# Two chained cross attentions: a pair's first-batch image outputs as products and sums on GpSimd

## The chip, the core and the metric

The kernel runs on one core of a Trainium2 chip. The core has engines that work side by side, each with its own queue that it takes in order: TensorE (PE in the profile, its weight loads PEld), VectorE (DVE), ScalarE (ACT), GpSimd (POOL) and SyncE (SP), which here issues nearly all transfers (DMAs). They wait for one another by semaphores. TensorE writes into PSUM, a small memory that is handed out here in eight equal tiles of 2 KB per partition; the other operands lie in SBUF, which has 128 partitions. The metric is the device time of one execution in microseconds (us).

## The reference

There are 64 batches of 256 tokens with 320 channels (20 heads of 16 channels), and for each batch 77 context rows of 512, of which the last 4 are image tokens for the second layer.

```python
# layer 0: plain cross attention over the 77 rows (and an image part that has no rows here)
out_text = _merge_heads(_attend(q, k, v, sm_scale))
x = out @ Wo.T + bo + x
# layer 1: 73 text rows and 4 image rows
probs_t = softmax(q @ k_t * scale)
text_out = probs_t @ v_t
qsem = l2norm(probs_t @ text_ehs)
sem = qsem @ l2norm(ip_ehs).T
probs_ip = softmax(q @ k_ip * scale + 0.5 * sem) * spatial_mask
ip_out = probs_ip @ v_ip
out = (text_out + ip_out) @ W_out + b_out + x
```

The change concerns `ip_out = probs_ip @ v_ip` and its addition to `text_out`: for each token and head, four weights times four value rows of 16 channels.

## The kernel before

**Pairs and units.** Two batches make a pair; there are 32 pairs. The 20 heads are split into 16 main ones, which fill two times 128 channels, and 4 last ones (64 channels), which are kept apart. A batch is worked off in five units of 128 tokens by 8 heads, so a pair has ten units (`NU`). The main loop (L1098) runs over steps `g`; step `g` belongs to pair `p = g // 10`, and `k = g % 10` is the number of the step that this text uses (step 0 to step 9). In each step layer 0 works on unit `g` and layer 1 on unit `g - 13` (`LAG`). So while layer 0 works on pair `p`, layer 1 ends batch 0 of pair `p - 1` in step 9 of `p`, and its image part runs in the steps of `p + 1`. This is why calls in the list of work carry `p - 2`.

**The order in a step.** Work is emitted in this order: work held for this step (`early`, and the ends of projections); the matmuls of the scores into one PSUM tile of four banks, `sc` (pool `psc`, one buffer), for `semantics` (L760, L766), `scores` of both layers (L646); work called `begin`, with the image matmuls' copies in step 8; on DVE the maxima and subtractions of both layers (`shifted`, L664 and L666), then `middle`; the transposes of layer 1's weights (`transposed`); the exponential of layer 0; `weighted` on DVE (L777, L780), the last reader of `sc` but one; the list `first`; layer 0's transposes; `sums_out` on ACT (L1092), the last reader of `sc` (it stands ahead of layer 0's transposes in steps 1 and 8); the exponentials of layer 1 (L677, L678); `normalize` (DVE L692 and L693, then POOL L697, which makes `parts`, read by PE in the next step); `later`; at the end of a batch `text_output`; the lists `second`; `attend`; and `third`. `fillers(k, p)` puts the other work into these lists: `first`, `second`, `third` and `begin` are its lists 0, 1, 2 and 3.

`keep_order` makes PE, ACT, DVE and POOL take their instructions in the order in which they were written. SP is held to it only in the first 13 steps; after that the framework's scheduler orders SP's transfers by when it thinks that buffers come free, and may issue them early.

**PSUM.** Besides `sc` there are two pools of two tiles each: `ptr` (tag `tr`) for transposes and `pms` (tag `ms`) for matmuls. A third tile of a pool has to wait until a reader, mostly an ACT copy, is done with the first.

**The image part of layer 1.** When a batch ends, `text_output` scales the text outputs by head on POOL (L884) into `an` as [token, head, channel], the last four heads into `an_last`. In the steps after it come `image_scores`, `image_shifted`, `image_exponential` and `image_weights`, which give the weights `iw` as [token, half of the tokens, head, image token]. `text_transposed` turns `an` into channels by token on PE (L846) and copies it into `aT` (ACT, L848); this is in step 0 for batch 0 and in step 5 for batch 1. For the image outputs, `image_values` loads the four rows of `v_ip` sixteen times, once per head (`vip`, 16 transfers a batch, steps 7 and 8), `place_image_values` masks them by head on POOL (L483, step 9); `image_transposed` turns the weights of both batches into rows by token (PE, L948, four transposes into one `ptr` tile `itr`, and the ACT copy L950 into `iwT`, step 7); `image_attend` multiplies both (PE, L960, into two `pms` tiles `ipv`, step 8), copies them to SBUF (ACT, L970) and adds them to `aT` (POOL, L972). The last four heads are done otherwise: `last_image_values` loads the rows broadcast over all partitions (`vlast`), and `last_image_outputs` makes four products and four sums on POOL (L857, L860). `project(1, p - 2)` and `project_last(1, p - 3)` then read `aT`, in step 9 and in step 0.

Other work that the prediction names: `value_rows` (`v_ps`, PE L381, ACT copy `vs` L382) makes the value rows of a block of 128 context rows; `keys` and `last_keys` (`k_ps`, `kl_ps`, ACT copies L339 and L351); `gram` (its transfers `g_rest`, L515); `project_last(0, p - 1)` in step 2 ends with DVE's L625, for which PE's `last_queries` (L573, `q_ps`) waits; `image_least` (`least`, L897) squares the sums on POOL at the end of a batch. In the last steps, when there is no layer 0 any more, `keep_busy` has PE do transposes that nobody reads.

Of the kernel before, what the change touches and what calls it, by code (L numbers as in the profile page):

```python
# [15 lines left out]
D = 16  # L16
# [49 lines left out]
def tile_two_cross_attentions(ctx: ExitStack, tc: tile.TileContext, a: dict, out: bass.AP):  # L66
# [350 lines left out]
    def place_values(l, p, b):  # L417
# [51 lines left out]
            rest0[:n].rearrange("p (i g) -> p i g", g=4).unsqueeze(3).broadcast_to([n, 2, 4, D]), ALU.mult,  # L469
        )  # L470

    def image_values(p, b):


        n, r0 = HT * NIP, (2 * p + b) * NIP
        vip = vips[p, b] = big.tile([n, 2 * P], F32, tag="vip", name=f"vip{p}_{b}", bufs=3)
        for h in range(HT):
            nc.sync.dma_start(vip[h * NIP : (h + 1) * NIP, :], vip_rows[r0 : r0 + NIP, : 2 * P])

# [345 lines left out]
    def text_output(p, b):  # L825

        sums = stats[p, b][1]
        rec = small.tile([P, 2 * H], F32, tag="rec", name=f"rec{p}_{b}", bufs=2)
        nc.vector.reciprocal(rec, sums[:, :, NIP + D])
        an = big.tile([P, 2, HT, D], F32, tag="an", name=f"an{p}_{b}", bufs=1)  # L830
        if b == 0:
            lasts[p] = big.tile([P, 2, 2, H - HT, D], F32, tag="an_last", name=f"an_last{p}", bufs=1)
        by_head(an, lasts[p][:, :, b], sums[:, :, NIP : NIP + D], rec)
        return an

    def text_transposed(p, b):

        an = made["an"]
        if b == 0:
            aTs[1, p] = channels("aT1", f"aT1_{p}", 1)  # L840
        main = aTs[1, p][0]
        for s in range(2):
            ps = ptr.tile([P, 4, P], F32, tag="tr", name=f"atr{p}_{b}{s}")
            t = an[:, s].rearrange("p h d -> p (h d)")
            for i in range(2):
                nc.tensor.transpose(ps[:, i, :], t[:, i * P : (i + 1) * P], ident)  # L846
            t0 = b * S + s * P
            nc.scalar.copy(main[:, :, t0 : t0 + P], ps[:, :2])  # L848

    def last_image_outputs(p, b):  # L850

        v = vips[p, b, "last"].rearrange("p t (h d) -> p t h d", d=D)
        w, to = weights[p, b, "last"], lasts[p][:, :, b]
        part = [P, 2, H - HT, D]
        for t in range(NIP):
            prod = small.tile(part, F32, tag="ip_last", name=f"ip_last{p}_{b}{t}", bufs=1)
            nc.gpsimd.tensor_tensor(  # L857
                prod, v[:, t].unsqueeze(1).broadcast_to(part), w[:, :, :, t].unsqueeze(3).broadcast_to(part), ALU.mult
            )
            nc.gpsimd.tensor_add(to, to, prod)  # L860
# [81 lines left out]
    def image_transposed(p):  # L942
        n = HT * NIP
        ps = ptr.tile([P, 4, P], F32, tag="tr", name=f"itr{p}")
        for b in range(2):
            w = weights[p, b].rearrange("p s h t -> p s (h t)")
            for s in range(2):
                nc.tensor.transpose(ps[:n, 2 * b + s, :], w[:, s], ident)  # L948
        wT = big.tile([n, S2], F32, tag="iwT", name=f"iwT{p}", bufs=1)
        nc.scalar.copy(wT, ps[:n].rearrange("p j t -> p (j t)"))  # L950
        return wT

    def image_attend(p):

        wT = made["wT"]
        both = [pms.tile([P, 512], F32, tag="ms", name=f"ipv{p}_{i}") for i in range(2)]
        for b in range(2):
            for i in range(2):
                rows = slice(i * QR, (i + 1) * QR)
                nc.tensor.matmul(  # L960
                    both[i][:, b * S : (b + 1) * S], vips[p, b][rows, i * P : (i + 1) * P],
                    wT[rows, b * S : (b + 1) * S], start=True, stop=True,
                )

        def out_of(i):
            main = aTs[1, p][0]
            if p == NP - 1:
                nc.vector.tensor_add(main[:, i, :], both[i], main[:, i, :])
                return
            nc.scalar.copy(t[:, i, :], both[i])  # L970
            if i:
                nc.gpsimd.tensor_add(main, t, main)  # L972

        t = big.tile([P, 2, S2], F32, tag="ip_out", name=f"ip_out{p}", bufs=1)
        return [lambda i=i: out_of(i) for i in range(2)]


# [2 lines left out]
    def fillers(k, p):  # L980
# [4 lines left out]
        def add(half, q, fn, *args):  # L985
            if 0 <= q < NP:
                f[half].append((fn, args))

        if k == 0:
# [3 lines left out]
                add(1, p, values, 0, p, 0)  # L993
            add(0, p - 1, gram, p - 1, 0)
            add(0, p - 3, project_last, 1, p - 3)
            add(2, p - 2, text_transposed, p - 2, 0)
            if p:
                add(2, p, place_values, 0, p, 0)
            add(2, p - 1, values, 1, p - 1, 0)
        elif k == 1:  # L1000
# [3 lines left out]
                add(1, p, place_values, 0, p, 0)  # L1004
            add(0, p - 1, project, 0, p - 1)
            add(1, p - 2, last_image_values, p - 2, 0)
            add(1, p - 1, place_gram, 0)
            add(1, p, keys_by_head, 0, p, 1)
            add(1, p - 1, keys_by_head, 1, p - 1, 0)
        elif k == 2:  # L1010
# [6 lines left out]
            add(2, p - 1, lambda: made["q"]())  # L1017
            add(1, p - 1, place_values, 1, p - 1, 0)
            add(1, p, values, 0, p, 1)
        elif k == 3:  # L1020
            add(0, p + 1, load_context, p + 1)
            add(0, p, lambda: last_queries(0, p)())
            if p == 0:
                add(1, p, image_keys, 0)
            add(1, p - 1, queries, 1, p - 1)
            add(1, p, place_values, 0, p, 1)
            add(1, p - 1, keys_by_head, 1, p - 1, 1)
        elif k == 4:
            if p == 0:
                add(0, p, image_keys, 1)  # L1030
            else:
                add(0, p, keys, 1, p, 0)
            add(1, p - 1, values, 1, p - 1, 1)
            add(1, p - 2, last_image_outputs, p - 2, 0)
            add(1, p + 1, queries, 0, p + 1)
        elif k == 5:
            if p == 0:
                add(0, p, image_keys, 2)
            add(0, p + 1, keys, 0, p + 1, 0)
            add(1, p - 1, gram, p - 1, 1)  # L1040
            add(2, p - 2, text_transposed, p - 2, 1)
            add(1, p - 2, last_image_values, p - 2, 1)
        elif k == 6:
            while len(made_rows) * P < min(NB, 2 * (p + 2)) * T:
                rows_todo.extend((len(made_rows), l) for l in range(2))
                made_rows.append(rows_todo[-1])
            for n in range(len(rows_todo) // 2):
                add(0, p, value_rows, *rows_todo.pop(0))
            if p == 0:
                add(0, p, image_norms)  # L1050
            else:
                add(1, p, keys, 1, p, 1)
            add(1, p, place_image_keys, p)
        elif k == 7:
            add(0, p + 1, keys, 0, p + 1, 1)
            add(1, p + 1, last_keys, p + 1)
            add(1, p - 2, lambda: made.update(wT=image_transposed(p - 2)))
            add(1, p - 2, last_image_outputs, p - 2, 1)
            add(1, p - 1, image_values, p - 1, 0)
            if p == 0:  # L1060
                add(1, p, image_rows)
        elif k == 8:
            while rows_todo:
                add(0, p, value_rows, *rows_todo.pop(0))
            add(1, p - 1, place_gram, 1)
            add(1, p + 1, keys_by_head, 0, p + 1, 0)
            add(1, p - 1, image_values, p - 1, 1)
            add(1, p - 1, place_values, 1, p - 1, 1)
            add(1, p - 2, last_transposed, p - 2)
            add(3, p - 2, lambda: held.update(i=lambda: image_attend(p - 2)))  # L1070
        else:
            add(0, p - 2, project, 1, p - 2)
            add(1, p + 1, values, 0, p + 1, 0)
            for b in range(2):
                add(1, p - 1, place_image_values, p - 1, b)
        return f

    rows_todo, made_rows = [], [0, 1]
# [19 lines left out]
    for g in range(NP * NU + LAG + 12):  # L1098
# [39 lines left out]
            new1 = (*last1, pts[1])  # L1138
        if now[0] and k != 5:
            exponential(0, g, *now[0])  # L1140
        if before1:
            prod = weighted(ps, *before1[:4])
        if g - NP * NU in (18, 19):
            keep_busy(6)
        for fn, args in first:
            fn(*args)
        if before1 and k in (1, 8):
            sums_out(ps)
        if last0:
            transposed(0, *last0)  # L1150
# [6 lines left out]
            keep_busy(8)  # L1157
        if now[0] and k == 5:
            exponential(0, g, *now[0])
        if before1 and k not in (1, 8):  # L1160
            sums_out(ps)
        if now[1]:
            exponential(1, g, *now[1])
# [4 lines left out]
        if before1:  # L1168
            q, b, u = before1[:3]
            nc.vector.tensor_reduce(eight(stats[q, b][2], u), prod, AX.X, ALU.add)  # L1170
            if ends:
                image_squares(q, b)
                made["an"] = text_output(q, b)
                later[g + 1] = [(image_scores, (q, b))]
                middle[g + 2] = (image_shifted, (q, b))
                later[g + 2] = [(image_exponential, (q, b))]
                early[g + 3] = [(image_weights, (q, b))]
        for fn, args in second:
            fn(*args)
        if last0:  # L1180
# [63 lines left out]
```

## Time and profile before

| what | value |
|---|---|
| time, median of 3 runs | 2580.65 us (2578.83 to 2582.64) |
| the profiled execution, its own time | 2582.37 us |
| its span in the profile | 2580.6 us |
| granted TensorE clock, mean | 0.996 |
| one pair of batches in the middle (1193.8 to 1270.0 us) | 76.2 us |
| in it, busy: PE, DVE, ACT, POOL | 75.5, 60.7, 46.8, 51.7 us |

In the profile a line such as `L697 POOL ... parts<-w,sm` names the engine, the line of the kernel, what is written and what is read. Groups have their total busy time, the mean length of one in ns, and the idle time of the engine just ahead of them with what ended it. The chain of work is followed back from the last instruction, at each step to what released it. In the list of waits a line gives who waited for whom, the total in us, how often, and the longest. Ends of matmuls are modelled, so PE can look busy while it is held up.

### The profile page before, as it was taken

Reading aid. Unit: us, or ns where it says so; the run is one execution under the profiler, and the core shown is the slowest. Engines: PE = TensorE matmul, PEld = TensorE weight load, DVE = VectorE, ACT = ScalarE, POOL = GpSimd, SP = SyncE. Lnnn points to the kernel's source line nnn. Section 1 sums busy time; section 2 is a strip of 40 time slices with the busy share of each in tenths; the row PEclk is TensorE's granted clock in tenths of the full one; section 3 lists DMA queues with packets and bytes.
Section 4 is the critical chain, followed back from the end, with each engine's and each line's share of the span. In section 5 each row is a group of like instructions: output and inputs, shape, how many; then the busy total and the mean of one; then the engine's idle time right before and its main releaser. Section 6 shows DMA issues by size and latency. Waiting matters only on the chain.

```text
span 2580.6 us, 74528 instructions
## 1 busy us (share of the span) xinstructions
PE 2514.9 (97%) x27178; PEld 2010.2 (78%) x27178; DVE 1954.0 (76%) x3609; ACT 1510.1 (59%) x3893; POOL 1653.7 (64%) x4026
## 2 busy tenths in 40 slices
PE   7999999999999999999999999999999999999898
PEld 6677778777787777788777787777787777787676
DVE  4577777878777778777777777777777777777764
ACT  3465665665665665566665566656565665566543
POOL 3466666676666676666666666666666666666653
PEclk9999999999999999999999999999999999999999
DMA  5212211122211121212122212122211122211000
GB/s 166 58 45 61 62 46 47 49 59 55 63 45 49 48 59 54 64 44 52 45 59 54 64 45 52 45 58 54 67 44 48 45 60 54 62 41 41 26 25 27
DMA packets 186405, 138.33 MB, mean 54 GB/s; under 512 B 81016, under 2 KB 164728, under 8 KB 186040
## 3 DMA queue, kind: packets, MB, share of 16 engines
q1 hardware_dynamic: 185176, 132.41, 19.0%
q8 instruction: 217, 3.56, 0.6%
q14 instruction: 148, 1.21, 0.2%
q10 hardware_dynamic: 864, 1.15, 0.1%
HBM read 95.56 MB, written 33.91 MB: 50 GB/s over the span
## 4 chain that ended last, share of the span: by engine, by line
PE 68%; DVE 16%; ACT 4%; POOL 3%; DMA 3%; SPq 3%; issue 3%; DVEq 0%; POOLq 0%; ACTq 0%
PE sc L760 10%; PE q_ps L537 8%; PE tr L710 8%; PE sc L646 6%; DVE w L666 5%; PE v_ps L381 4%; DVE mx L664 4%; PE o_ps L537 4%; PE sc L766 4%; PE k_ps L336 4%; PE q_ps L546 3%; DVE prod L777 2%; PE pv L794 2%; DVE x L606 2%; PE pv L799 2%
## 5 line engine op out<-in xcount | busy, mean ns | idle before, releaser
L664 DVE TENSOR_REDUCE mx<-sc 128x8 f32<-128x584 f32 (+1 forms) x640 | 497.2, 777 | 439.3 <-PE sc L646 439.2
L697 POOL TENSOR_TENSOR parts<-w,sm 128x512 f32<-128x512 f32 (+1 forms) x640 | 440.5, 710 | 370.1 <-DVE sm L693 194.2
L666 DVE TENSOR_TENSOR w<-sc,mx 128x616 f32<-128x616 f32 x640 | 511.9, 800 | 66.6 <-ACT kT L339 0.5
L710 PE MATMUL tr<-ident,parts 128*128 128x128 f32 x2560 | 408.4, 282 | 8.1 <-POOL parts L697 3.8
L717 ACT COPY pt<-tr 128x512 f32<-128x512 f32 x320 | 187.5, 586 | 378.9 <-PE tr L710 376.2
L760 PEld LDWEIGHTS sc<-gv,pt 64*128 64x128 f32 x5120 | 319.5, 187 | 71.9 <-ACT sums L1092 44.1
L710 PEld LDWEIGHTS tr<-ident,parts 128*128 128x128 f32 x2560 | 284.9, 141 | 115.8 <-issue 71.4
L760 PE MATMUL sc<-gv,pt 64*128 64x94 f32 x5120 | 353.1, 277 | 12.8 <-ACT sums L1092 10.3
L674 ACT ACTIVATE w<-w 128x616 f32<-128x616 f32 x320 | 231.0, 722 | 151.9 <-DVE w L666 143.0
L692 DVE TENSOR_REDUCE sm<-w 128x8 f32<-128x616 f32 x320 | 250.9, 784 | 13.9 <-ACT w L674 13.9
L646 PE MATMUL sc<-kbd,q 32*128 32x154 f32 x5120 | 248.4, 306 | 1.0 <-ACT q L591 1.0
L537 PE MATMUL q_ps<-x,wq 128*128 128x256 f32 x1024 | 233.5, 381 | 3.3 <-ACT kT L339 3.3
L537 PE MATMUL o_ps<-aT,wo 128*128 128x256 f32 x1024 | 232.6, 380 | 0.0
L1170 DVE TENSOR_REDUCE nrm<-prod 128x8 f32<-128x584 f32 x320 | 227.1, 710 | 0.4
L777 DVE TENSOR_TENSOR prod<-sc,parts 128x512 f32<-128x512 f32 x320 | 217.9, 681 | 4.0 <-PE sc L766 4.0
L1092 ACT COPY sums<-sc 128x168 f32<-128x168 f32 x320 | 96.5, 302 | 199.8 <-DVE prod L780 198.9
L537 PEld LDWEIGHTS q_ps<-x,wq 128*128 128x128 f32 x1024 | 190.0, 191 | 27.6 <-ACT kT L339 4.3
L537 PEld LDWEIGHTS o_ps<-aT,wo 128*128 128x128 f32 x1024 | 190.3, 191 | 23.5 <-issue 0.2
L677 ACT ACTIVATE parts<-w 128x512 f32<-128x512 f32 x320 | 207.2, 647 | 0.0
L646 PEld LDWEIGHTS sc<-kbd,q 32*128 32x128 f32 x5120 | 187.0, 186 | 5.9 <-issue 4.8
L736 ACT COPY pt<-tr 128x512 f32<-128x512 f32 x256 | 150.1, 586 | 63.0 <-PE tr L710 62.7
L381 PE MATMUL v_ps<-wv,cf 128*128 128x320 f32 (+1 forms) x624 | 182.1, 438 | 0.0
(147 smaller groups left out, 4788.0 us busy)
## 6 DMA issues: line engine op xcount, KB each, us to landing
vip<-vip_rows SPq DMA_DIRECT2D x1024, 4.0 KB
out_dram<-x SPq DMA_DIRECT2D x64, 256.0 KB
x<-in_x_dram SPq DMA_DIRECT2D x31, 512.0 KB
v_rows<-vs SPq DMA_DIRECT2D x38, 320.0 KB
vm<-v_rows SPq DMA_DIRECT2D x152, 80.0 KB
ct<-in_ctx_dram SPq DMA_DIRECT2D x32, 308.0 KB
cf<-in_ctx_dram SPq DMA_DIRECT2D x38, 256.0 KB
g_rest<-gram_rest SPq DMA_DIRECT2D x512, 0.5 KB
```

The lines of the kernel that those rows point to most:

```text
L381: nc.tensor.matmul(ps[:n, :C], cfs[i][:, k, :n], wv[l][:, k, :], start=(k == 0), stop=(k == KE - 1))
L537: nc.tensor.matmul(ps[b][:, m, :], w[:, k, m * P : (m + 1) * P], main[:, k, b * S : (b + 1) * S], start=(k == 0 and m == 0), stop=False,)
L646: nc.tensor.matmul(ps[:, r, 2 * T * l : 2 * T * (l + 1)], q[rows, b, :] if part == 2 else q[rows, t0 : t0 + P], kbd[rows, part].rearrange( ...
L664: nc.vector.tensor_reduce(mx, sc[:, :, :, :nt], AX.X, ALU.max)
L666: nc.vector.tensor_tensor(w, sc, mx.unsqueeze(3).broadcast_to([P, 4, 2, T]), ALU.subtract)
L674: nc.scalar.activation(w, w, AF.Exp, scale=SCALE)
L692: nc.vector.tensor_reduce(sm, w, AX.X, ALU.add)
L697: nc.gpsimd.tensor_tensor(two[:, 8 * t0 : 8 * t1].rearrange("p (h t) -> p h t", h=8), w[:, :, t0:t1], sm.unsqueeze(2).broadcast_to([P, 8, ...
L710: nc.tensor.transpose(ps[:, i, :], flat[:, i * P : (i + 1) * P], ident)
L760: nc.tensor.matmul(ps[:, i % 2 * 2 + j, at : at + GV], pt[half_rows, i, :], gv[b][half_rows, part, i, :], start=start and i < 2, stop=False,)
L777: nc.vector.tensor_tensor(prod[:, :, :, :M], sm[:, :, :, :M], w[:, :4].rearrange("p (e a) j t -> p (a j) e t", e=2), ALU.mult)
L1170: nc.vector.tensor_reduce(eight(stats[q, b][2], u), prod, AX.X, ALU.add)
```

## The change

For batch 0 of each pair, the image outputs of the 16 main heads are no longer made by matmuls. `head_values` loads one row of `v_ip` broadcast over 128 partitions (`vt`, two buffers, 128 KB a load, four loads a pair). `head_products` multiplies it on POOL by the weights of that image token, over [token, half, head, channel] (128x512), and `head_sum` adds the product to `an`. This goes on in steps 2, 3 and 4: token 0 and its sum early in step 2, the product of token 1 at the end of step 2, sum 1, product 2, sum 2 and product 3 in step 3, sum 3 in step 4. `an` has two buffers, since batch 0's is now kept until step 7, where `text_transposed` of batch 0 comes (before, step 0); `aT` is now opened by batch 1 in step 5. `last_image_outputs` of batch 0 does two image tokens in step 4 and two in step 5, and `last_image_values` of batch 1 moves behind them. `image_values`, `place_image_values`, `image_transposed` and `image_attend` are left for batch 1 alone. Two orders change besides: in step 2 the list `first` runs ahead of `weighted`, and in step 6 `sums_out` runs ahead of layer 0's transposes.

```diff
+    def head_values(p, t):
+        r = 2 * p * NIP + t
+        v = vips[p, 0, t] = small.tile([P, 2 * P], F32, tag="vt", name=f"vt{p}_{t}", bufs=2)
+        nc.sync.dma_start(v, vip_rows[r : r + 1, : 2 * P].broadcast_to([P, 2 * P]))
...
-        vip = vips[p, b] = big.tile([n, 2 * P], F32, tag="vip", name=f"vip{p}_{b}", bufs=3)
+        vip = vips[p, b] = big.tile([n, 2 * P], F32, tag="vip", name=f"vip{p}_{b}", bufs=2)
...
-        an = big.tile([P, 2, HT, D], F32, tag="an", name=f"an{p}_{b}", bufs=1)
+        an = big.tile([P, 2, HT, D], F32, tag="an", name=f"an{p}_{b}", bufs=2)
...
-        return an
+        ans[b] = an
+
+    ans = {}
+
+    def head_products(p, t):
+        full = [P, 2, HT, D]
+        prod = made["ip"] = big.tile(full, F32, tag="ip_out", name=f"ip{p}_{t}", bufs=1)
+        nc.gpsimd.tensor_tensor(
+            prod, vips[p, 0, t].rearrange("p (h d) -> p h d", d=D).unsqueeze(1).broadcast_to(full),
+            weights[p, 0][:, :, :, t].unsqueeze(3).broadcast_to(full), ALU.mult,
+        )
+
+    def head_sum():
+        nc.gpsimd.tensor_add(ans[0], ans[0], made["ip"])
 
     def text_transposed(p, b):
-        an = made["an"]
-        if b == 0:
+        an = ans[b]
+        if b == 1:
             aTs[1, p] = channels("aT1", f"aT1_{p}", 1)
...
-    def last_image_outputs(p, b):
+    def last_image_outputs(p, b, tokens=range(NIP)):
...
-        for b in range(2):
-            w = weights[p, b].rearrange("p s h t -> p s (h t)")
-            for s in range(2):
-                nc.tensor.transpose(ps[:n, 2 * b + s, :], w[:, s], ident)
-        wT = big.tile([n, S2], F32, tag="iwT", name=f"iwT{p}", bufs=1)
-        nc.scalar.copy(wT, ps[:n].rearrange("p j t -> p (j t)"))
+        w = weights[p, 1].rearrange("p s h t -> p s (h t)")
+        for s in range(2):
+            nc.tensor.transpose(ps[:n, s, :], w[:, s], ident)
+        wT = big.tile([n, S], F32, tag="iwT", name=f"iwT{p}", bufs=1)
+        nc.scalar.copy(wT, ps[:n, :2].rearrange("p s t -> p (s t)"))
...
-        for b in range(2):
-            for i in range(2):
-                rows = slice(i * QR, (i + 1) * QR)
-                nc.tensor.matmul(
-                    both[i][:, b * S : (b + 1) * S], vips[p, b][rows, i * P : (i + 1) * P],
-                    wT[rows, b * S : (b + 1) * S], start=True, stop=True,
-                )
+        for i in range(2):
+            rows = slice(i * QR, (i + 1) * QR)
+            nc.tensor.matmul(both[i], vips[p, 1][rows, i * P : (i + 1) * P], wT[rows, :], start=True, stop=True)
...
         if k == 0:
-            add(2, p - 2, text_transposed, p - 2, 0)
...
         elif k == 1:
+            for t in range(2):
+                add(1, p - 2, head_values, p - 2, t)
...
         elif k == 2:
+            add(2, p - 2, head_products, p - 2, 1)
+            add(2, p - 2, head_values, p - 2, 3)
         elif k == 3:
...
+            add(1, p - 2, head_sum)
+            add(1, p - 2, head_products, p - 2, 2)
+            add(1, p - 2, head_sum)
+            add(1, p - 2, head_products, p - 2, 3)
         elif k == 4:
...
-            add(1, p - 2, last_image_outputs, p - 2, 0)
+            add(1, p - 2, head_sum)
+            add(1, p - 2, last_image_outputs, p - 2, 0, range(2))
...
         elif k == 5:
...
             add(2, p - 2, text_transposed, p - 2, 1)
-            add(1, p - 2, last_image_values, p - 2, 1)
+            add(2, p - 2, last_image_outputs, p - 2, 0, range(2, NIP))
+            add(2, p - 2, last_image_values, p - 2, 1)
...
         elif k == 7:
...
             add(1, p - 2, lambda: made.update(wT=image_transposed(p - 2)))
             add(1, p - 2, last_image_outputs, p - 2, 1)
-            add(1, p - 1, image_values, p - 1, 0)
+            add(2, p - 2, text_transposed, p - 2, 0)
...
-            for b in range(2):
-                add(1, p - 1, place_image_values, p - 1, b)
+            add(1, p - 1, place_image_values, p - 1, 1)
...
+        if k == 2:
+            for fn, args in first:
+                fn(*args)
         if before1:
             prod = weighted(ps, *before1[:4])
...
-        if before1 and k in (1, 8):
+        if before1 and k in (1, 6, 8):
             sums_out(ps)
...
+                if b == 0:
+                    early[g + 3] += [(head_products, (q, 0)), (head_sum, ()), (head_values, (q, 2))]
```

More of the change, by code (lines that the diff above doesn't have):

```diff
@@ L854, in last_image_outputs @@
         part = [P, 2, H - HT, D]
-        for t in range(NIP):
+        for t in tokens:
             prod = small.tile(part, F32, tag="ip_last", name=f"ip_last{p}_{b}{t}", bufs=1)
@@ L955, in image_attend @@
         wT = made["wT"]
-        both = [pms.tile([P, 512], F32, tag="ms", name=f"ipv{p}_{i}") for i in range(2)]
-        for b in range(2):
-            for i in range(2):
-                rows = slice(i * QR, (i + 1) * QR)
-                nc.tensor.matmul(
-                    both[i][:, b * S : (b + 1) * S], vips[p, b][rows, i * P : (i + 1) * P],
-                    wT[rows, b * S : (b + 1) * S], start=True, stop=True,
-                )
+        both = [pms.tile([P, 512], F32, tag="ms", name=f"ipv{p}_{i}")[:, :S] for i in range(2)]
+        for i in range(2):
+            rows = slice(i * QR, (i + 1) * QR)
+            nc.tensor.matmul(both[i], vips[p, 1][rows, i * P : (i + 1) * P], wT[rows, :], start=True, stop=True)
         def out_of(i):
-            main = aTs[1, p][0]
+            main = aTs[1, p][0][:, :, S:]
             if p == NP - 1:
-                nc.vector.tensor_add(main[:, i, :], both[i], main[:, i, :])
+                nc.vector.tensor_add(main[:, i], both[i], main[:, i])
                 return
@@ L972, in out_of @@
                 nc.gpsimd.tensor_add(main, t, main)
-        t = big.tile([P, 2, S2], F32, tag="ip_out", name=f"ip_out{p}", bufs=1)
+        t = big.tile([P, 2, S], F32, tag="ip_out", name=f"ip_out{p}", bufs=1)
         return [lambda i=i: out_of(i) for i in range(2)]
@@ L1144, in tile_two_cross_attentions @@
             keep_busy(6)
-        for fn, args in first:
-            fn(*args)
-        if before1 and k in (1, 8):
+        if k != 2:
+            for fn, args in first:
+                fn(*args)
+        if before1 and k in (1, 6, 8):
             sums_out(ps)
@@ L1159, in tile_two_cross_attentions @@
             exponential(0, g, *now[0])
-        if before1 and k not in (1, 8):
+        if before1 and k not in (1, 6, 8):
             sums_out(ps)
@@ L1172, in tile_two_cross_attentions @@
                 image_squares(q, b)
-                made["an"] = text_output(q, b)
+                text_output(q, b)
                 later[g + 1] = [(image_scores, (q, b))]
```

## The prediction

> **What bounds the kernel now.** I read the page's busy shares and its chain first, then the chain and each engine's timeline over one pair of batches in the middle (1194 to 1270 us), then the waits and the groups by shape.
>
> ```profile
> PE 2514.9 (97%) x27178; PEld 2010.2 (78%) x27178; DVE 1954.0 (76%) x3609; ACT 1510.1 (59%) x3893; POOL 1653.7 (64%) x4026
> PE 68%; DVE 16%; ACT 4%; POOL 3%; DMA 3%; SPq 3%; issue 3%; DVEq 0%; POOLq 0%; ACTq 0%
> ```
>
> TensorE (PE) is the bound on average, but the chain is only 68% PE, so steps differ. A step begins with its first `sc` matmul, and the starts of these groups give the steps' lengths, medians over pairs 4 to 30, steps 0 to 9: 8.02, 7.69, 7.91, 9.29, 8.58, 6.42, 6.82, 6.88, 6.75, 7.82 us. Every other pair repeats them within a few hundredths, except where a step carries a second block of value rows (steps 6 and 8, up to 8.58 and 8.90, in about one pair of five).
>
> There are two kinds of step. In the short ones (5, 6, 8) the only `sc` tile is held until VectorE (DVE) has read it for the fifth time and ScalarE (ACT) has copied the sums: 2.1 us of `sc` matmuls, 3.9 of DVE, 0.3 of ACT and gaps, about 6.5. In the others PE has more than that to do. Step 7 of the next pair, in the chain, is PE from end to end:
>
> ```profile
> 1277.40 1.13 PE sc L760 x16
> 1278.54 0.38 PE sc L766 x8
> ...
> 1281.79 1.05 PE kl_ps L346 x8
> 1282.85 0.51 PE itr L948 x4
> 1283.35 0.57 PE pv L794 x8
> 1283.92 0.43 PE pv L799 x8
> 1284.36 1.06 PE sc L760 x16
> ...
> 1286.38 0.85 PE ipv L960 x8
> ```
>
> The columns are start, length, what. `itr` is the image weights' transposes and `ipv` the image matmuls; the change halves both. ACT at the end of the same step 7, one pair earlier:
>
> ```profile
> 1207.41 0.30 ACT L1092 COPY sums<-sc 128x168 f32<-128x168 f32 x1 [0.71 <-DVE prod L780]
> 1207.61 0.64 ACT L677 ACTIVATE parts<-w 128x512 f32<-128x512 f32 x1
> 1208.15 0.25 ACT L678 ACTIVATE parts<-w 128x72 f32<-128x72 f32 x1
> 1208.31 0.57 ACT L351 COPY kl<-kl_ps 64x154 f32<-64x154 f32 x2
> 1208.90 0.58 ACT L950 COPY iwT<-itr 64x512 f32<-64x512 f32 x1
> ```
>
> ACT has no gap from 1207.41 on, and the copy that empties `itr` ends near 1209.48, while PE has gone into step 8 at 1208.15. Today nobody in step 7 minds that.
>
> **The change, part by part.** I count per pair, from 1201.27 (step 7's `sc`) on.
>
> *Step 7, PE.* Half of `itr` goes: 0.51 / 2 = 0.25 us. Four transposes of the first batch come at the end of the step (0.59 us, the `atr` row below). That alone makes +0.34. But the transposes need two PSUM tiles of the pool `ptr`, which has two slots: `transposed` of layer 0 takes both, `itr` the first that comes free, the first `atr` tile the other, and the second `atr` tile the slot of `itr`. So PE waits in its queue until ACT has done the `iwT` copy. That such a wait is real in this kernel is seen in the other two-slot pool:
>
> ```profile
> PEld v_ps L381 <- ACT ip_out L970: 6.1, 29, 0.2
> ```
>
> The `v_ps` matmuls have no data from `ip_out`; they wait 29 times for the slot. When does `iwT` end? What stands ahead of it on ACT is unchanged: sums (bound to DVE's `prod`, which ends 6.09 after `sc`), two exponentials, two `kl` copies; so it starts at 1208.90 again. Its length at 64x256 is not in the trace: between 0.29 (half of 579 ns) and 0.58 (as now); I take 0.37, since copies of 128x256 take 366 to 390 ns (L818, L869). So 1209.27; 0.05 for the semaphore; two transposes and the change of weights 0.45 (four take 0.59, of which 0.17 is the gap ahead of `sc`). Step 8 starts at 1209.77 instead of 1208.15: +1.62. PE would have arrived at this transpose near 1208.25, so about 1.05 of it is waiting. Queued behind it on PE is the next `sc`, and behind that all of DVE's chain.
>
> *Step 6's copies.* `sums_out` moves ahead of layer 0's transposes. In 6 the sums wait for DVE anyway (0.30 us idle), so nothing comes earlier; the two `pt`/`pr` copies and the exponentials come 0.7 us later. ACT idles 1.74 us before step 7's `pt` copy, which hides this; only the exponential of the image scores lies near a reader (`imx`, DVE) and may cost 0 to 0.08. I put 0.03. Step 7: +1.65, with bounds +0.34 and +1.95.
>
> *Step 8.* Half of `ipv` goes (0.43 PE), the ACT copies `ip_out` fall from 1.07 to some 0.6, and the GpSimd (POOL) addition L972 from 2.37 to 1.28. The step is bound by the `sc` chain: 6.75 now against 6.5 to 6.55, because the `vs` copy holds ACT 0.2 us past `prod`. So −0.20; in the fifth of pairs with two row blocks it is PE's, −0.43. Mean −0.25 (0 to −0.43).
>
> *Step 0.* Text transposes of the first batch leave it.
>
> ```profile
> 1230.16 0.66 PE L846 MATMUL atr<-ident,an 128*128 128x128 f32 x4
> 1230.75 1.13 PE L760 MATMUL sc<-gv,pt 64*128 64x94 f32 x16
> 1244.74 0.62 PE L799 MATMUL pv<-pr,vr 104*32 104x256 f32 x8
> 1245.71 0.66 PE L573 MATMUL q_ps<-x,wq 128*64 128x128 f32 x8 [0.35 <-DVE x L625]
> ```
>
> The sums of that step were out at 1229.94, so `sc` was ready 0.8 us before PE: the whole 0.59 is gained. Step 1 behind it has PE work without a gap, with 0.9 us between its sums and the next `sc`, so it passes the gain on.
>
> *Step 2.* `first` runs before `weighted`, so DVE does L625 before `prod`, and PE's 0.35 us before `q_ps` goes. `prod` and the sums come 0.40 later (1245.98 against PE's 1245.95): −0.30, between 0 and −0.35.
>
> *POOL.* Added: four products and four sums of 128x512.
>
> ```profile
> L697 POOL TENSOR_TENSOR parts<-w,sm 128x512 f32<-128x512 f32 x320 | 336.5, 1051 | 370.1 <-DVE sm L693 194.2 <-ACT parts L678 122.6 <-ACT gram L506 38.3
> L860 POOL TENSOR_TENSOR an_last<-an_last,ip_last 128x128 f32<-128x128 f32 x256 | 116.9, 457 | 20.1
> L972 POOL TENSOR_TENSOR aT<-ip_out,aT 128x1024 f32<-128x1024 f32 x31 | 73.4, 2369 | 1.4 <-ACT ip_out L970 1.4
> ```
>
> A product by L697 is 1.05. A sum lies on the line through L860 and L972: 457 + 384 × 2.13 = 1.28. Together 9.3; off come 1.1 of L972 and one L483 (0.6): +7.6, from 51.7 to 59.3 us of 76.2. Place by place: in step 2 POOL is done with the image weights at 1244.0 and `parts` starts at 1246.76, so 2.33 fit with 0.2 for `att`; the product behind the placed values ends near 1252.6, before `parts` at 1253.61; in step 3, POOL idles 4.43 us from 1257.7 to 1262.1, where two products and two sums take 4.7. There `least` and `parts` may come 0.3 late; PE needs these `parts` at 1267.7, so nothing. Step 4 swaps four small operations (1.9 us) for one sum (1.3); in step 5 they stand in the idle 2.15 before L921. Cover for all of it is PE's distance of a step to each `parts`; were it gone, each microsecond late is one.
>
> POOL work does not slow DVE: 347 of `w` (L666) ran beside a POOL instruction and 175 beside none, 800 ns both; `sm` (L692) took 784 both ways. L901, whose two tensors both lie in SBUF, takes 345 beside POOL and 200 without. The Trainium skill, "SBUF — State Buffer", section "Who interferes with whom", says a DVE instruction with two SBUF inputs contends with a GpSimd instruction that reads SBUF, one with at most one such input not; by it, too, only L901 would be touched. Against moving such work speaks "GPSIMD Engine Reference", section "Engine selection": two-input elementwise work is some 2 times slower there than on VectorE. By that, an estimate, the eight take 2 x 681 ns (`prod`, 128x512, on DVE), 10.9 us in place of 9.3; the rows (1051 to 681) say 1.5 times for the product, and the sum goes by the rows.
>
> *Queues.* SP loses 16 `vip` issues (8 take 3.13 us, so 6.3) and gains four (1.6). The first two loads have free buffers since step 3 of the pair before. Loads of tokens 2 and 3 wait for products at about 1245.1 and 1252.6, and are needed near 1259 and 1261. A load like it (`vlast`, issued at 1213.35) has its last packet at 1216.37, 3.0 us. `last_image_values` waits a step longer, to about 1199.7, behind eight `g_rest` issues (to 1204.5), lands by 1207.7 and is read at 1209.8. Cost 0, if SP's order is the program's. SP is not held to that order.
>
> *Tail.* POOL's small operations of step 5 now stand before L921 (+0.9), the transposes are on the path (+0.6), half of `ipv` goes (−1.1): +0.4 once.
>
> Sum: 1.65 − 0.25 − 0.59 − 0.30 = +0.51 per pair; 30 pairs run step 7 in full, +15.3, and the tail: +15.7. The profiled execution took 2582.37 (span 2580.6), so it would take 2598; it lies 1.7 above the median of the runs, which gives 2580.65 + 15.7 = 2596.
>
> **The rivals.**
> *No slot wait, faster.* If the `iwT` copy is no hindrance (ACT gets to it earlier, or the tile gets another slot), step 7 grows by 0.34 and the sum is −0.80 a pair, −24: 2557. It decides below a growth of 1.14 in step 7, that is where `iwT` is out 0.5 us earlier. For it: PE's gains are plain rows. Against: two slots, and ACT without a gap from the sums to `iwT`.
> *They cancel.* The wait is half of what I say, or DVE takes up more of it in step 8: −5 to +5.
> *A load comes late, slower still.* If SP issues `vlast` behind the `kl` transfers (1209.9), it lands at about 1213; POOL starts step 7's last outputs 3 us late, and PE's `ltr` in step 8, which by then has 2.1 us of margin, waits some 1 us: +30, 2627. For it: SP already waits 401 us at L489 for `ip_last`. Against: it has work before `kl`.
> *POOL becomes the bound.* At 59.3 of 76.7 us it isn't; only a place could be too tight, and the tightest (step 3) has 3.6 us to PE.
>
> **How the numbers follow.** My forecast has 0.60 and its own range is 2586 to 2608 (step 7 between +1.3 and +1.95). No slot wait 0.21, cancelling 0.08, late load 0.11. A measurement here tells about 0.2% (5 us) from none. Faster is the second case and a little of the third, 0.22; same 0.09; slower 0.69. A range that leaves out no more than 2 in 10 takes in half of the faster case and ends above the forecast's own: 2556 to 2612.
>
> **What would show it.** Right: step 7 near 8.5 us with a PE wait of about 1 us at `atr`, ended by `iwT`; step 8 near 6.5, step 0 near 7.4, step 2 near 7.6 with no wait for L625. Wrong: `atr` starting right behind `pv`; POOL's products waiting for a `vt` load; `sc` waiting for POOL's `least` chain.

## The result, and the profile after

The changed kernel takes 2600.5 us (median of 4 runs, 2597.46 to 2602.34) against 2581.64 us (4 runs, 2578.83 to 2583.97) of the kernel before: a ratio of 1.0078, with a 95% interval of 1.0063 to 1.0093. It is slower by 0.8%. The prediction was 2596 us, in a range of 2556 to 2612. The profiled execution took 2602.34 us with a span of 2600.6, that is 20.0 us more span than before.

The page of the changed kernel, busy shares and chain (lines of the code moved by 6 to 28: L760 is now L766, L897 is L918):

```profile
PE 2497.0 (96%) x26986; PEld 1993.9 (77%) x26986; DVE 1954.7 (75%) x3609; ACT 1496.2 (58%) x3893; POOL 1899.5 (73%) x4250
PE 56%; DVE 20%; ACT 10%; POOL 5%; DMA 4%; issue 3%; SPq 2%; DVEq 0%; POOLq 0%; ACTq 0%
```

TensorE (PE) has 18 us less to do and GpSimd (POOL) 246 us more, yet neither sum gives the time. The shift in the chain points to where it comes from: PE's share falls from 68% to 56%, and ScalarE's (ACT) rises from 4% to 10%. PE waits for ACT at places where it had work before.

The steps, measured from the first `sc` matmul of one to that of the next, show where. The medians are over pairs 4 to 30; the last column adds up the differences of the two profiled executions over steps `g` = 20 to 319.

| step | before, us | after, us | after less before, all pairs, us |
|---|---|---|---|
| 0 | 8.02 | 7.27 | −21.5 |
| 2 | 7.91 | 7.60 | −8.8 |
| 4 | 8.58 | 8.58 | −5.4 |
| 5 | 6.42 | 6.42 (six of 7.4 to 10.3) | +16.4 |
| 7 | 6.88 | 8.41 | +46.3 |
| 8 | 6.75 | 6.59 | −7.4 |
| 1, 3, 6, 9 | 7.69, 9.29, 6.82, 7.82 | the same | −0.1 |

The start adds 1.7 and the end takes 1.3: together 20 us. Step 7 alone costs more than the change gains elsewhere, and its PE timeline shows how (start, length, instruction; in brackets the idle time and who ended it):

```profile
750.90 0.38 PE L968 MATMUL itr<-ident,iw 128*64 128x128 f32 x2
751.21 0.64 PE L800 MATMUL pv<-pt,v 128*32 128x256 f32 x8
751.66 0.62 PE L805 MATMUL pv<-pr,vr 104*32 104x256 f32 x8
752.21 0.44 PE L867 MATMUL atr<-ident,an 128*128 128x128 f32 x2
753.54 0.44 PE L867 MATMUL atr<-ident,an 128*128 128x128 f32 x2 [0.88 <-ACT iwT L970]
753.90 1.13 PE L766 MATMUL sc<-gv,pt 64*128 64x94 f32 x16
```

The first two text transposes run behind `pv`; the next two wait 0.88 us for the `iwT` copy, and the next step's `sc` stands behind them. This step began at 745.49. ACT at the same time:

```profile
751.63 0.30 ACT L1116 COPY sums<-sc 128x168 f32<-128x168 f32 x1 [0.71 <-DVE prod L786]
751.83 0.64 ACT L683 ACTIVATE parts<-w 128x512 f32<-128x512 f32 x1
752.36 0.26 ACT L684 ACTIVATE parts<-w 128x72 f32<-128x72 f32 x1
752.52 0.58 ACT L351 COPY kl<-kl_ps 64x154 f32<-64x154 f32 x2
753.12 0.37 ACT L970 COPY iwT<-itr 64x256 f32<-64x256 f32 x1
```

From the sums on ACT has no gap, as before, and `iwT` ends at 753.49, 8.00 us after the step's start. In the list of waits the same is summed up over the kernel, beside the wait for L625 (now L631), which has shrunk from 25.3 us:

```profile
PEld atr L867 <- ACT iwT L970: 32.8, 30, 1.1
PEld q_ps L579 <- DVE x L631: 12.6, 31, 0.4
```

The six long steps 5 are another matter. Pair 10, POOL, from the `parts` of its step 3 to the `least` of its step 4 (POOL runs behind PE here: by `sc`, step 4 begins at 800.15 and step 5 at 808.73):

```profile
798.18 1.38 POOL L703 TENSOR_TENSOR parts<-w,sm 128x512 f32<-128x512 f32 x2 [0.48 <-ACT parts L684]
803.08 0.72 POOL L455 TENSOR_TENSOR v<-vm,half 128x320 f32<-128x320 f32 x1 [3.52 <-DMA vm<-v_rows]
...
805.76 1.27 POOL L855 TENSOR_TENSOR an<-an,ip 128x512 f32<-128x512 f32 x1
807.11 1.09 POOL L848 TENSOR_TENSOR ip<-vt,iw 128x512 f32<-128x512 f32 x1
808.29 1.27 POOL L855 TENSOR_TENSOR an<-an,ip 128x512 f32<-128x512 f32 x1
809.63 1.10 POOL L848 TENSOR_TENSOR ip<-vt,iw 128x512 f32<-128x512 f32 x1
810.70 0.26 POOL L918 TENSOR_TENSOR least<-sums 128x40 f32<-128x40 f32 x1
```

POOL waits 3.52 us for a load of value rows, `vm`. Then come the placing, the sums and products of the change (L855, L848), and only then `least`. VectorE (DVE), ACT and PE, a line of each timeline, pass the delay on:

```profile
811.00 0.20 DVE L922 SCALAR_TENSOR_TENSOR nrm<-least,nrm 128x40 f32<-128x40 f32 x1 [3.18 <-POOL least L918]
...
811.23 0.24 ACT L926 ACTIVATE nrm<-nrm 128x40 f32<-128x40 f32 x1 [2.65 <-DVE nrm L922]
812.89 1.05 ACT L597 COPY q<-q_ps 128x512 f32<-128x512 f32 x2
...
813.51 1.32 PE L336 MATMUL k_ps<-ct,wk 128*128 128x154 f32 x8 [2.09 <-ACT q L597]
```

ACT can copy the queries only behind the norms, and PE's `k_ps` needs the slots that the queries hold. The late load itself is older than the change, and has not become later by it. The list of waits has it ten times in the kernel before (first line) and seven times in the changed one:

```profile
POOL v L455 <- DMA vm<-v_rows: 27.9, 10, 6.5
POOL v L455 <- DMA vm<-v_rows: 19.5, 7, 4.0
```

In the kernel before, the 4.4 us in which POOL had nothing to do at the end of step 3 took up most of it; only two pairs were visibly longer (9.54 and 13.12 us in step 4).

### The profile page after: what moved, and what is told of

It is laid out like the page before. It is cut to its first block, busy times and chain, and to the rows that moved or that the text cites. A ratio compares the mean times of both kernels' runs of the same rounds, so it can differ in the third digit from the quotient of the medians.

```text
span 2600.6 us, 73747 instructions
## 1 busy us (share of the span) xinstructions
PE 2497.0 (96%) x26986; PEld 1993.9 (77%) x26986; DVE 1954.7 (75%) x3609; ACT 1496.2 (58%) x3893; POOL 1899.5 (73%) x4250
## 3 DMA queue, kind: packets, MB, share of 16 engines
q8 instruction: 215, 3.52, 0.6%
## 4 chain that ended last, share of the span: by engine, by line
PE 56%; DVE 20%; ACT 10%; POOL 5%; DMA 4%; issue 3%; SPq 2%; DVEq 0%; POOLq 0%; ACTq 0%
PE sc L766 9%; DVE w L672 7%; PE q_ps L543 7%; PE tr L716 6%; PE sc L652 5%; DVE mx L670 5%; PE o_ps L543 4%; PE sc L772 3%; DVE prod L783 3%; PE k_ps L336 3%; PE v_ps L381 2%; ACT w L680 2%; PE q_ps L552 2%; PE pv L800 2%; DVE x L612 2%
## 5 line engine op out<-in xcount | busy, mean ns | idle before, releaser
L766 PEld LDWEIGHTS sc<-gv,pt 64*128 64x128 f32 x5120 | 319.5, 187 | 82.7 <-ACT sums L1116 52.5
L766 PE MATMUL sc<-gv,pt 64*128 64x94 f32 x5120 | 353.1, 277 | 26.9 <-ACT sums L1116 22.1
```

The lines of the kernel that those rows point to most:

```text
L766: nc.tensor.matmul(ps[:, i % 2 * 2 + j, at : at + GV], pt[half_rows, i, :], gv[b][half_rows, part, i, :], start=start and i < 2, stop=False,)
```

## The experiments

Theory S: the second text-transposed tile of step 7 waits for the slot of the two-slot pool `ptr` that the `iwT` copy empties. Theory L: a late `vm` load, once hidden by POOL's idle time in step 3, now reaches PE. The rivals: PE has too many transposes in step 7 (W), POOL is too full in general or the long steps are chance (N). Times are set against runs of the kernel before on the same chip.

| run | median, us | ratio to before, interval | step 5 | step 6 | step 7 |
|---|---|---|---|---|---|
| changed kernel | 2600.5 | 1.0078, 1.0063 to 1.0093 | six long | 6.82 | 8.41 |
| iwT copy ahead of `kl` copies | 2601.03 | 1.0084, 1.0067 to 1.0101 | six long | 6.82 | 8.37 |
| products first in step 3 | 2627.5 | 1.0190, 1.0175 to 1.0206 | 6.42 | 6.82 | 8.42 |
| before, two orders alone | 2572.6 | 0.9971, 0.9962 to 0.9981 | 6.42 | 6.82 | 6.88 |
| no products | 2580.65 | 1.0006, 0.9997 to 1.0015 | 6.42 | 6.82 | 8.41 |
| text in step 6 | 2554.72 | 0.9905, 0.9890 to 0.9920 | six long | 6.85 | 6.72 |
| text in step 6, sums early | 2577.6 | 0.9996, 0.9987 to 1.0005 | six long | 7.89 | 6.72 |
| `place_values` last in step 3 | 2587.2 | 1.0030, 1.0018 to 1.0042 | 6.47 | 6.82 | 8.41 |
| text in step 6, `place_values` last | 2537.94 | 0.9843, 0.9826 to 0.9859 | 6.47 | 6.86 | 6.72 |
| loads cut at sixteens | 2588.02 | 1.0037, 1.0025 to 1.0048 | 6.42 | 6.82 | 8.42 |
| text in step 6, loads cut | 2540.16 | 0.9845, 0.9829 to 0.9862 | 6.42 | 6.85 | 6.72 |

The six long steps 5 stand in the same pairs (6, 10, 11, 20, 21 and 25) in all four runs that have them, so they are not chance.

### The copy of iwT earlier on ACT

```diff
-            add(1, p + 1, last_keys, p + 1)
             add(1, p - 2, lambda: made.update(wT=image_transposed(p - 2)))
+            add(1, p + 1, last_keys, p + 1)
```

> The changed kernel with one order altered in step 7: the image weights' transposes and their copy iwT come ahead of last_keys, so on ScalarE iwT no longer stands behind the two kl copies (0.59 us). Theory S (the second text-transposed tile waits for the slot that iwT empties): step 7 falls by 0.59 from 8.41 to 7.82 us, the wait of atr for iwT from about 1.1 to 0.5, the other steps stay, 30 pairs give -18 us, about 2583. Rival W (step 7 is longer because TensorE has more transposes there, or because GpSimd is fuller): the same transposes are there, step 7 stays at 8.41 and the time near 2600.

A miss: step 7 fell by 0.04 us only. The four text transposes run in one go, but the wait has moved to the image transposes ahead of them:

```profile
748.72 0.27 PE L717 MATMUL rtr<-ident,parts 128*104 128x128 f32 x1
750.02 0.38 PE L968 MATMUL itr<-ident,iw 128*64 128x128 f32 x2 [1.03 <-ACT pt L742]
750.24 1.22 PE L346 MATMUL kl_ps<-ct,wk_last 128*128 128x154 f32 x8
```

`itr` follows layer 0's transposes at once now, and their `pt` copy has not emptied the slot. I had left out that `last_keys` on PE stood between the two and gave ACT time. It is the same shortage of slots at another place. By its time the run came out as W expected it, and the number that I gave for S fails, since I looked at one of the pool's waits and not at the other; against W speaks here only this wait in the trace.

### The text transposes in another step

```diff
         elif k == 6:
...
             add(1, p, place_image_keys, p)
+            add(2, p - 2, text_transposed, p - 2, 0)
...
-            add(2, p - 2, text_transposed, p - 2, 0)
...
-        if before1 and k in (1, 6, 8):
+        if before1 and k in (1, 8):
...
-        if before1 and k not in (1, 6, 8):
+        if before1 and k not in (1, 8):
```

> The changed kernel with the first batch's text transposes in step 6 in place of step 7, and the sums' copy of step 6 behind layer 0's transposes as in the kernel before. In step 6 no third tile of the pool stands between, and both slots are emptied by 6.2 us after the step's sc, before TensorE comes to these transposes at 6.45. Theory S: no slot wait in either step; step 7 falls from 8.41 to 6.6 (6.88 of before less 0.25), step 6 rises from 6.82 to 7.1 (9.1 where there are two row blocks), the long steps 5 stay; -43 us, about 2557. Rival W (the four transposes themselves cost it): step 7 falls by 0.6 only and the time to about 2590.

As expected by S: 2554.72 us, 24 below the kernel before. Step 7 is 6.72, and the four transposes, the same ones, cost step 6 only 0.03 us in the median (0.28 had been expected), since PE waited there for the sums; in the six pairs with two row blocks they cost 0.44 (8.57 to 9.01). They run in one go, with no wait:

```profile
735.35 0.60 PE L867 MATMUL atr<-ident,an 128*128 128x128 f32 x4
```

The next run keeps the sums' copy early in step 6, as the changed kernel has it; that is the same diff without its changes to `before1 and k`.

> As the run with the text transposes in step 6, but with the sums' copy of step 6 ahead of layer 0's transposes, as in the changed kernel. ScalarE then empties the two slots of layer 0's transposes only after the sums, at 7.25 and 7.42 us after the step's sc. Theory S: step 6 has a slot wait of about 0.8 us and is near 7.85 in place of 7.1, step 7 stays at 6.6; about 2580. Rival W: no difference to the other order, 2557 or 2590 as there.

Step 6 is 7.89 us and step 7 stays at 6.72. The slot wait is there:

```profile
739.10 1.16 PE L336 MATMUL k_ps<-ct,wk 128*128 128x146 f32 x8
741.08 0.66 PE L867 MATMUL atr<-ident,an 128*128 128x128 f32 x4 [0.82 <-ACT pt L742]
741.67 0.80 PE L766 MATMUL sc<-gv,pt 64*128 64x94 f32 x10
```

The work is equal in both runs; only when ACT empties the slots differs, and it is worth 23 us (2577.6 to 2554.72). W is out: not the transposes cost the time, but the emptying of the tiles that they need.

### The products left out, or in another order

In one run the loads, products and sums are taken away (all calls of `head_values`, `head_products` and `head_sum`), and so the first batch's main image outputs.

> The changed kernel without the loads, products and sums of the first batch's main heads: their image outputs are left out, all else is as in the changed kernel. Theory S with L: step 7 stays at 8.41 with its wait for iwT, steps 0, 2 and 8 stay at 7.27, 7.60 and 6.59, the long steps 5 are gone, about 2585. Rival W (fuller GpSimd holds TensorE up in step 7 or elsewhere): step 7 falls towards 7.2 and the time to 2560 or less.

Step 7 stays at 8.41 with its waits for `iwT`, the long steps 5 are gone though `vm` is nearly as late, and the time, 2580.65, is that of the kernel before:

```profile
PEld atr L867 <- ACT iwT L970: 33.6, 31, 1.1
POOL v L455 <- DMA vm<-v_rows: 17.5, 7, 4.1
```

So the products cost some 19 us (1.0078 against 1.0006). Of the 21.6 us between the two profiled executions, 17.5 lie in step 5 and 3.9 behind step 319, at the kernel's end. What remains of the change, gains and slot wait, cancels.

```diff
+            add(1, p - 2, head_sum)
+            add(1, p - 2, head_products, p - 2, 2)
+            add(1, p - 2, head_sum)
+            add(1, p - 2, head_products, p - 2, 3)
             add(1, p, place_values, 0, p, 1)
             add(1, p - 1, keys_by_head, 1, p - 1, 1)
-            add(1, p - 2, head_sum)
-            add(1, p - 2, head_products, p - 2, 2)
-            add(1, p - 2, head_sum)
-            add(1, p - 2, head_products, p - 2, 3)
```

> The changed kernel with one order altered on GpSimd in step 3: the two sums and two products stand ahead of place_values and keys_by_head. Theory L (in about one pair of five the vm load is up to 4 us late; before, GpSimd's idle time in step 3 took that up, now products and sums fill it, and least, the norms and the queries' copies of step 5 come late): step 5 is 6.42 in all pairs, the six long ones (7.4 to 10.3 us, 15.8 us in all above 6.42) are gone, -16 us, about 2585; the late vm is then covered by the products. Rival N (the long steps 5 are chance of one execution, or GpSimd's load in general): they stay, 2600.

Half right. The long steps 5 are gone, as L says, but step 4 grows from 8.58 to 9.89 in every pair, because `keys_by_head` reads the tile `kT`, which ACT has to write anew in step 4; PE's `q_ps` then waits for a slot behind that copy:

```profile
ACT kT L339 <- POOL kbd L367: 63.3, 30, 2.4
PEld q_ps L543 <- ACT kT L339: 42.6, 29, 1.8
```

So only the instruction that waits for the load should go last:

```diff
-            add(1, p, place_values, 0, p, 1)
             add(1, p - 1, keys_by_head, 1, p - 1, 1)
             add(1, p - 2, head_sum)
             add(1, p - 2, head_products, p - 2, 2)
             add(1, p - 2, head_sum)
             add(1, p - 2, head_products, p - 2, 3)
+            add(1, p, place_values, 0, p, 1)
```

> The changed kernel with place_values (which waits for the vm load) behind keys_by_head, the two sums and two products on GpSimd in step 3; keys_by_head, whose lateness lengthened step 4 by 1.3 us when it stood behind the products, is first. Theory L: step 5 is 6.42 in all pairs as with the products ahead of both, and step 4 stays at 8.58; -16 us, about 2585. Rival: another reader of what place_values makes is early enough to be held up, then step 4 or a later step grows in every pair and the time stays near or above 2600.

2587.2 us, no long step 5, step 4 unchanged; step 5 is 6.47 in every pair. L holds: the same POOL work in another order costs 12 us less (1.0030 against 1.0078).

### Both together

> Both: text transposes in step 6 with the old order of its sums' copy, and place_values last in step 3. If slot wait and late load are all that made the changed kernel slower, the gains add: 2600 - 43 - 16, about 2541, which is 38 us below the kernel before. If they overlap or a new wait comes, more than 2550.

2537.94 us, 0.9843 of the kernel before: the two causes are separate and add up. This is faster than both kernels of this case.

### The two orders alone

```diff
+        if k == 2:
+            for fn, args in first:
+                fn(*args)
         if before1:
             prod = weighted(ps, *before1[:4])
...
-        if before1 and k in (1, 8):
+        if before1 and k in (1, 6, 8):
```

> The kernel before with only the two orders altered: first ahead of weighted in step 2, sums_out ahead of layer 0's transposes in step 6. By the prediction step 2 falls by 0.30 from 7.91 to 7.60, step 6 stays at 6.82, 31 pairs give -9.5 us, about 2571. Rival: step 2's gain in the changed kernel comes from the shorter step 0 ahead of it or from what moved on GpSimd, then no change here.

2572.6 us, 0.9971. Step 2 falls to 7.65 (7.60 in some pairs), step 6 stays at 6.82. Nearly all of the gain of step 2 (7.7 us in 30 pairs, of 8.8) belongs to the order of DVE's two instructions and not to anything else in the change.

### Why the load is late

Value rows lie in blocks of 128, and a batch's 64 rows are loaded in two pieces where a block ends between them. In the six pairs with a long step 5 the pieces have 41 and 23, 47 and 17, or 43 and 21 rows. Each row is loaded twice, so a batch's load is 128 packets of 1280 bytes. In the late pair above, the trace's packet records have nearly all of them (126) one behind the other: from 796.0 to 802.5 one starts every 52 ns and lasts 55 ns, 9 or 10 in each half microsecond. In the pair before it, with uncut loads, all 128 start within 1.6 us, 59 and 52 of them in the two half microseconds from 719.0.

```diff
             n = min(P - r, end - at)
+            n = n // 16 * 16 if 16 < n < M else n
             o = at - r0 - t0
```

> The changed kernel with one thing altered: where a batch's 64 value rows lie in two blocks, a load of more than 16 rows is cut into one whose number of rows is a multiple of 16 and one with the rest. The pairs with long steps 5 are those whose second batch is cut into 41 and 23, 47 and 17 or 43 and 21 rows; with 45 and 19, 49 and 15 or 39 and 25 rows the step is 6.42. Theory P (the load is late because such a load runs on one or a few of the 16 DMA engines, the largest number up to 16 that divides its rows): the loads come in time with no other order on GpSimd, step 5 is 6.42 to 6.5 in all pairs, -16 us, about 2585. Rival Q (the load is late because SP issues it late or the transfers are many): more issues make it later, 2600 or more.

2588.02 us with no long step 5 (the longest in pairs 2 to 30 is 6.77): P's forecast holds and Q's does not, for more issues made the loads earlier. With the text in step 6:

> The same cut of the loads, with the text transposes in step 6 and the old order of its sums' copy. By P it ends where the run with place_values last and the text in step 6 did, near 2538, or a few us below, since place_values is back in its place (step 5 at 6.42 in place of 6.47). By Q near 2555.

2540.16 us, level with the version that places the values last.

## Why the prediction was right, and where not

**The slot wait, right.** "Step 8 starts at 1209.77 instead of 1208.15" is a growth of 1.62, with the copies of step 6 1.65, and 1.53 was measured. The copy that ends 8.00 after `sc` came out to the hundredth; its length, taken as 0.37 between 0.29 and 0.58, is 365 ns. What was too long by 0.1 is the stretch from there to `sc`: I put 0.50, it took 0.41 (753.49 to 753.90). Per pair and in total: +49.5 forecast, +46.3 measured.

**Steps 8 and 2, right.** −0.25 and −0.30 forecast per pair; −7.4 us in 30 pairs and −0.31 in the median came. The wait for L625 did not go, as the sign of being right had it, but was halved (25.3 to 12.6 us). The order in step 6 was put at 0.03 and showed nothing.

**Step 0, too small.** −0.59 forecast, −0.75 measured in the median (8.02 to 7.27), −21.5 in all. The 0.59 are the four transposes themselves. The 0.16 more came off ahead of where they stood: in the medians PE's `o_ps` (L621) begins 3.35 us after the step's `sc` before the change and 3.25 after it, and the first `pv` 5.56 and 5.39. Why is not shown.

**POOL, wrong in one term.** The lengths were right (1111 ns a product and 1274 a sum, against 1.05 and 1.28), and so was the fit place by place: in an ordinary pair `least` starts at 730.69, with POOL busy from 721.70 on. The step that failed is "There `least` and `parts` may come 0.3 late; PE needs these `parts` at 1267.7, so nothing". It reckons with a pair in which the load is in time. The list of waits of before, which I had read, showed the load late ten times by up to 6.5 us; the 4.43 us of idle time in step 3 were its cover, and I spent them. The prediction has every pair repeat its steps within a few hundredths except for steps 6 and 8; the two late pairs, with 9.54 and 13.12 us in step 4, were lost in the medians. I also followed `least` to `parts` only, and not to the norms and ACT's copies of the queries. It is worth +16.4 in step 5, of which 5.4 come off again in step 4, where two late pairs had paid before: +11 net, which with a step 0 and a step 7 that came out 7 us better makes up the 4 us by which 2600.5 lies above 2596. That the number came so close is in part luck, since these errors have opposite signs.

**The rivals.** "No slot wait, faster" did not come to pass, but a kernel with that wait removed came close to its number: 2554.72 against 2557. That is partly luck, too: step 7, which the transposes had left, fell by 0.16 in place of growing by 0.34, and the long steps 5, which the rival did not have, took 19.5 us back. "A load comes late" was the right kind of trouble with the wrong load: `vlast` was in time except for one wait of 2.1 us, `vm` was not. POOL as the bound fell with the run without products: up to step 319 its work cost next to nothing except behind that load. At the kernel's end it costs some 4 us: behind step 319 come 118.6 us with the products and 114.8 without.

**DVE beside a busier POOL, right.** With 246 us more POOL work `w` still takes 800 ns and `sm` 784, while L922 (L901 before), which reads two tensors in SBUF, went from 338 to 403 ns. This agrees with the Trainium skill, "SBUF — State Buffer", section "Who interferes with whom".

## What to carry to other kernels

When work moves to another place, count the tiles of each small pool that are alive there and ask when the reader that empties each one gets to it; here the wait for a slot was set by that reader's queue, not by data. An engine's idle time that is named as cover should be measured in its worst pass, not in a typical one, since it may already be paying for something that is late now and then. Where both kinds of trouble were removed, the same change that had cost 0.8% gained 1.6%. Most of that is not the removed matmuls: of the 44.4 us between the profiled executions of that run and of the kernel before, 21.5 stand in step 0, which the text transposes left, and 8.8 in step 2 with its changed order; steps 7 and 8, which lost the matmuls, give 12.1. Whether the transposes could have moved without the offload was not run.

## What the runs showed of the hardware that I had not expected

A load of 41, 43 or 47 rows of 1280 bytes is several times slower than one of 64 rows, or one cut into 32 and a rest: POOL waited up to 4.0 us for it in the changed kernel, and in the pair whose packets were read, with 47 and 17 rows, they took 6.5 us in place of 1.6, about a quarter as many per microsecond. That fits the Trainium skill, "DMA: Bandwidth & Descriptors", section "Why a DMA increments its semaphore by 16 and not by 1": a transfer from SP's queue is spread over the largest number of DMA engines up to 16 that divides the slowest dimension larger than one on both of its sides; worked out for 41, 43, 47 or 17 rows, that is one. How many engines a load used was not seen here directly, though packets that start one every 52 ns and last 55 are what one engine would give; shown is that cutting it into multiples of 16 rows and a rest removed the delay.

The regular gap at `atr` is also what "Perfetto Trace Analysis", section "Optimization Strategy", says of consistent bubbles: on an engine that should be saturated they can mean that SBUF or PSUM has no room for the next tile. Here it was 0.9 us of PE in each of 30 pairs, 25.7 us in all, and the tiles were PSUM's.
